# Rows gathered as three bf16 parts in a GCN and GAT kernel, from chunk 28 of pass 1 and in all of pass 2

## The chip, the core and the metric

The kernel runs on one core of a Trainium2 chip. The metric is the device time of one execution in microseconds (us), the median over the runs. Data lie in HBM; SBUF (128 partitions) and PSUM are the core's own memories. TensorE (PE) multiplies, VectorE (DVE) and ScalarE (ACT) work elementwise, GpSimd (POOL) issues the indirect DMAs that gather rows, and SyncE (SP) and ACT issue the other DMAs.

## What is computed

12500 nodes have 256 features each, and 200000 edges go from `src` to `dst`, sorted by `dst`. Two graph convolutions are followed by an output product, and then by a mix over four heads:

```python
def _gcn_conv(x, W, b, src, dst, n):        # src, dst with a self loop for each node
    h = x @ W
    dinv = where(deg > 0, rsqrt(deg), 0.0)
    msgs = h[src] * (dinv[src] * dinv[dst])[:, None]
    return segment_sum(msgs, dst, n) + b

h = relu(layernorm(x))
h = h @ W_pre + b_pre
h = relu(_gcn_conv(h, W1, b1, src, dst, n))          # pass 1
h = relu(_gcn_conv(h, W2, b2, src, dst, n))          # pass 2
x = x + h @ W_post + b_post
xt = (relu(layernorm(x)) @ weight).reshape(-1, 4, 64)
alpha = softmax(leaky_relu(alpha_l[src] + alpha_r[dst], 0.01), axis=1)
out = x + mix of xt[dst] over the heads with alpha   # of the first n edges, broadcast to the heads
```

Everything is float32.

## The kernel before

`fast_path` does the work; a general path behind it is entered only when the edges are too uneven. The instructions of each engine run in the order in which the Python code emits them.

**Tables.** A first stage (to about 130 us) writes `table1` to HBM: one row of 260 float32 for each node, 256 values, the node's scale and padding (`D1 = 260`). Pass 1 gathers rows of `table1` and writes `table2` (256 float32 a row). Pass 2 gathers rows of `table2`.

**A pass.** `convolve` does one pass. The edges are cut into 112 chunks (`NCH`) of 14 tiles (`J`) of 128 edges; there are 1563 tiles, and the last chunk has 9. For a tile, GpSimd issues one indirect DMA (L1374) that brings the 128 rows of the edges' sources into `got`, and TensorE multiplies them by a one-hot matrix (`hots[c]`, made by DVE in `one_hots`, L1241) into the sum `acc` of the chunk (tile `facc`, L1382). A float32 matmul is two instructions on PE here. At a chunk's end `close` copies the sum (`fsums`, L1276), turns it on PE, and adds it into a window of nodes `buf` (L1293). When all edges of a node tile of 128 are in, `shift` hands it to `finish`: `finish1` in pass 1, `finish2` in pass 2, for 98 node tiles (`NT`) each.

**Delayed steps.** `finish` returns a list of `(offset, step, fills)`. A step is emitted that many edge tiles later, so that PE need not wait for what comes before it. Near a pass's end (`near`, the last three chunks) the steps follow each other at one tile each. `finish1` has two steps: `d` multiplies by the folded weights, `e` applies the relu into `o` and stores it to `table2` from ACT's queue (L1422, L1423). `finish2` has nine: `d` to `h` give the node's output row and its normalized form, `i` (L1514) turns it, `k` copies it, `q` multiplies by the attention weights, `r` stores the results to `table_l`, `table_e` and `table_r`.

**Gather buffers.** A buffer (`fgot`) holds one chunk: 14 gathers. Pass 1 has five, pass 2 four. The first four chunks of pass 1 (`raw`) come from an earlier gather of `x`. A pool gives out the buffer that was released first, and the first gather into it waits for the last reader. Besides, the DMAs of GpSimd share eight semaphores in turn, so that a gather waits until the one eight before it has landed.

**Where the passes meet.** The first chunk of pass 2 (`lacking`) reads only the table's first 96 node tiles, so that it can start early; what it lacks is added by `late_sums` (L1267). That function makes two blocks of one-hots of the sources with DVE in a buffer of the gather pool (`froms`), and multiplies them by the one-hots of the targets on PE, 14 tiles for each of two node tiles, after the second edge tile. Before its first tile, pass 2 loads three broadcast rows of indices (`to_all`, L1567 and L1593), turns them into one-hots (L1572, L1595), and loads and turns the first node rows (`self`, L1200, L1206).

**The last stage.** After pass 2, 98 gathers of 16 bytes a row (`fal`, L1662) bring the attention terms, and `mix` does the softmax and the output.

Of the kernel before, what the change touches and what calls it, by code (L numbers as in the profile page):

```python
# [17 lines left out]
P = 128  # L18
# [395 lines left out]
def fast_path(  # L414
# [56 lines left out]
    table1 = dram.tile([NT * P, D1], F32, name="ftable1")  # L471
    table2 = dram.tile([NT * P, D], F32, name="ftable2")
    kept_x = dram.tile([NT * P, D], F32, name="kept_x")

# [677 lines left out]

    def convolve(ep, table, stride, width, ahead, with_sum, psum, prepare, finish, lacking=False,
                 raw=(), rows_p=None):

# [83 lines left out]
        def one_hots(h, to):  # L1239
            n = to.shape[1]  # L1240
            nc.vector.tensor_tensor(h, iota_p[:, None, :].to_broadcast([P, n, P]),  # L1241
                                    to[:, :, None].to_broadcast([P, n, P]), ALU.is_equal)

        def hot_of(c):

            n = nj[c]
            h = ep.tile([P, J, P], F32, name="fhot", bufs=3)
            one_hots(h[:, :n, :], to_0 if lacking and c == 0 else to_t[:, c, :n])
            return h

        def new_rows_of():
            if with_sum:
                return new_got()
            return rows_p.tile([P, J, stride], F32, name="fgot", bufs=ahead)

        def late_sums():

            h = ep.tile([P, J, P], F32, name="fhot", bufs=3)
            one_hots(h, to_t[:, 0, :])
            froms = new_rows_of()  # L1260
            assert stride == TW * P
            for i in range(TW):
                one_hots(froms[:, :, i * P:(i + 1) * P], from_0[:, i, :])
            px = psum.tile([P, KC, P], F32, name="fpt", bufs=1)
            for i in range(TW):
                for j in range(J):
                    nc.tensor.matmul(px[:, i, :], froms[:, j, i * P:(i + 1) * P], h[:, j, :],  # L1267
                                     start=(j == 0), stop=(j == J - 1))
            many = work.tile([P, KC, P], F32, name="fz", bufs=2)
            nc.scalar.activation(many, px, AF.Copy)  # L1270
            return many, [load_rows((NT - TW + i) * P, P) for i in range(TW)]

        def close(c, acc, t):
# [3 lines left out]
            v = {}  # L1277
            near = c + 3 >= NCH

# [19 lines left out]
            def shift(now):  # L1299
# [31 lines left out]
                for i, (o, step, fills) in reversed(list(enumerate(steps))):  # L1331
                    then = at(now + (i + 1 if near else o), lambda _, step=step: step(), fills, then)
                state["w"] += 1
# [31 lines left out]
        for t, (c, j) in enumerate(tiles):  # L1365
            if j == 0:
                acc = psum.tile([P, width], F32, name="facc", bufs=2 if not with_sum else 3)

            if j == 0:
                gots = (raw + [spare])[c] if raw and c <= len(raw) else new_rows_of()  # L1370
            got = gots[:, j, :]
            some = lacking and c == 0
            if c >= len(raw):
                nc.gpsimd.indirect_dma_start(  # L1374
                    out=got, out_offset=None, in_=table[:(NT - TW) * P, :] if some else table[:],
                    in_offset=bass.IndirectOffsetOnAxis(
                        ap=src_0[:, j:j + 1] if some else src_t[:, c, j:j + 1], axis=0))
            if j == 2 and some:
                late = late_sums()
            if j == (5 if some else 2) and c + 1 < NCH:  # L1380
                hots[c + 1] = hot_of(c + 1)
            nc.tensor.matmul(acc, hots[c][:, j, :], got[:, :width], start=(j == 0),  # L1382
                             stop=(j == nj[c] - 1 and not some))
            if some and j == nj[c] - 1:
# [5 lines left out]
            if c + 1 < len(raw):  # L1390
                raw_ahead(c + 1, j)
            run(t)
        run()
# [16 lines left out]
    def finish1(work, psum, w, buf, sbuf, fs):  # L1410
# [9 lines left out]
        def e():  # L1420
            o = work.tile([P, D], F32, name="fo", bufs=3)
            nc.scalar.activation(o, v["po"], AF.Relu, scale=dinv2[:, w:w + 1])  # L1422
            nc.scalar.dma_start(table2[w * P:(w + 1) * P, :], o)  # L1423
            if w == 8:
                late_weights(late, attn)
                first_chunk()
            if w == 9:
                check_chunks(late, psum)

        return [(6, d, fills(w, "fpo")), (10, e, None)]  # L1430

    with tc.tile_pool(name="psum1", bufs=1, space=PSUM) as psum, \
# [4 lines left out]
        convolve(ep, table1, D1, D + 1, 4, True, psum, lambda w: prepare1(work, w),  # L1437
                 lambda w, b, s, pre, _: finish1(work, psum, w, b, s, pre), raw=raw,
                 rows_p=late)
    ring.close()  # L1440
# [23 lines left out]
    def finish2(work, psum, w, buf, pre, bias):  # L1464
# [65 lines left out]
        def r():  # L1530
# [8 lines left out]
            if w < XW:  # L1539
                nc.scalar.dma_start(table_r[w * P:(w + 1) * P, :], xa[:, :DR])  # L1540

        steps = [(6, d, fills(w, "fpz")), (8, e, None), (12, f, fills(w, "fpo")), (14, g, None),
                 (16, h, None), (20, i, fills(w, "fpt")), (22, k, None),
                 (26, q, fills(w, "fpx")), (28, r, None)]
        t = w - FROM
        if 0 <= t < J:
# [11 lines left out]

            steps += [(32, ends, "fpx"), (34, copied, None)]
        return steps  # L1560
# [20 lines left out]
    with tc.tile_pool(name="psum2", bufs=1, space=PSUM) as psum, \  # L1581
            tc.tile_pool(name="fwork2", bufs=2) as work, \
            tc.tile_pool(name="edges2", bufs=1) as ep, \
            tc.tile_pool(name="fgots2", bufs=1) as rows_p:
        ep.tile([P, 320], F32, name="apart")
        for c in range(EARLY):
# [7 lines left out]
        for i in range(LW):  # L1594
            nc.vector.tensor_scalar(hot_l[i], from_all, float((NT - LW + i) * P), lane,  # L1595
                                    op0=ALU.subtract, op1=ALU.is_equal)
        convolve(ep, table2, D, D, 4, False, psum, lambda w: prepare2(work, w),
                 lambda w, b, s, pre, bias: finish2(work, psum, w, b, pre, bias), True,
                 rows_p=rows_p)

# [152 lines left out]
```

## Time and profile before

| what | us |
|---|---|
| median of 3 runs | 4152.92 (4147.09 to 4158.49) |
| the profiled execution | 4146.65, of which the span of instructions is 4144.8 |
| first gather of pass 1, first of pass 2, last of pass 2 (start) | 130.35, 2024.51, 3983.19 |
| first `fal` gather, last `fal` gather (start) | 4002.20, 4125.64 |
| busy in the span: PE, DVE, ACT, POOL | 3094.9, 1139.5, 491.0, 3105.1 |
| mean granted TensorE clock | 0.80 |

The profile names a group of instructions by line, engine, operation and `output<-inputs`. "Idle before" is the time in which the engine stood still ahead of these instructions, and the arrow names what ended it; `issue` means that nothing that the profile shows was waited for. Times in a timeline count from the span's start. The profiled execution lies 6.27 us below the median of the runs.

### The profile page before, as it was taken

The numbers are of one execution on the slowest core, as the hardware profiler recorded it, in microseconds if no ns is written. First come the engines' busy times: TensorE is split into PE (matmuls) and PEld (weight loads), VectorE is DVE, ScalarE is ACT, GpSimd is POOL, SyncE is SP. The second block draws the span as 40 slices with busy tenths as digits, with TensorE's granted clock in tenths as the row PEclk, the third lists the DMA queues.
The fourth block names the chain that finished last, engine by engine and source line by source line (L and its number), as shares of the span: only waits on it lengthen the run. The fifth ranks groups of instructions, "written<-read, shape, count | busy, mean of one in ns | idle before, by whom it ended". The sixth has DMA issues, their size and how long they took to land. (4 is left out here: it accounts for less than half of the span.)

```text
span 4144.8 us, 32267 instructions
## 1 busy us (share of the span) xinstructions
PE 3094.9 (75%) x10600; PEld 1972.5 (48%) x10600; DVE 1139.5 (27%) x2421; ACT 491.0 (12%) x1233; POOL 3105.1 (75%) x3299
## 2 busy tenths in 40 slices
PE   6697887877777878788577777777777777777774
PEld 5464444444444444444365545554555545544452
DVE  8532111111111111111232222222222222222338
ACT  5400000000000000000011111111111111111122
POOL 8677777777777777777777777777777777777766
PEclk8688778788788787777698888888888888888876
DMA  9644444444444444444544445555455445554556
GB/s 278 190 125 123 118 120 120 123 120 120 120 122 120 120 120 122 117 120 120 149 125 134 129 128 128 128 132 128 127 128 132 128 128 127 129 126 129 132 167 201
DMA packets 327419, 554.57 MB, mean 134 GB/s; under 512 B 96301, under 2 KB 224836, under 8 KB 327244
## 3 DMA queue, kind: packets, MB, share of 16 engines
q0 software_dynamic: 153520, 414.16, 38.2%
q1 hardware_dynamic: 127878, 121.99, 9.8%
q10 hardware_dynamic: 45846, 16.27, 1.6%
q8 instruction: 87, 1.43, 0.1%
q14 instruction: 88, 0.72, 0.1%
HBM read 498.89 MB, written 53.21 MB: 133 GB/s over the span
## 5 line engine op out<-in xcount | busy, mean ns | idle before, releaser
L1374 POOL DMA_INDIRECT fgot<-ftable,fsrc_t x3056 | 2892.1, 946 | 948.7 <-issue 885.3
L1382 PE MATMUL facc<-fgot,fhot 128*128 128x257 f32 (+1 forms) x6252 | 2336.0, 494 | 888.1 <-DMA fgot<-ftable,fsrc_t 845.9
L1382 PEld LDWEIGHTS facc<-fgot,fhot 128*128 128x128 f32 x6252 | 1261.1, 231 | 1803.3 <-DMA fgot<-ftable,fsrc_t 1371.6
L1293 DVE TENSOR_TENSOR buf<-buf,fturn 128x256 f32 x224 | 94.4, 422 | 1627.2 <-PE fturn L1206 1296.8
L1241 DVE TENSOR_TENSOR fhot<-iota_p,to_t 128x1792 f32<-128x1792 f32 x224 | 448.9, 2004 | 4.5 <-PE fpt L1267 4.4
L1479 DVE SCALAR_TENSOR_TENSOR fy<-rb,fb2c,fpz 128x128 f32<-128x128 f32 x194 | 58.8, 345 | 718.5 <-PE fpz L1472 717.5
L1276 ACT ACTIVATE fsums<-facc 128x257 f32<-128x257 f32 (+1 forms) x224 | 85.9, 383 | 1146.0 <-PE facc L1382 1134.5
L1493 DVE SCALAR_TENSOR_TENSOR fx<-fpo,fdinv,fxb 128x256 f32<-128x256 f32 x97 | 46.9, 484 | 506.6 <-PE fpo L1488 506.6
L1417 PE MATMUL fpo<-wf,buf 128*128 128x256 f32 x388 | 156.9, 549 | 0.3 <-DVE buf L1293 0.3
L1422 ACT ACTIVATE fo<-fpo,fdinv 128x256 f32<-128x256 f32 x97 | 45.9, 473 | 754.0 <-PE fpo L1418 752.2
L1417 PEld LDWEIGHTS fpo<-wf,buf 128*128 128x128 f32 x388 | 113.8, 294 | 29.1 <-DVE buf L1293 0.8
L1472 PE MATMUL fpz<-buf,fwb 128*128 128x128 f32 x776 | 117.2, 300 | 0.0
L1488 PE MATMUL fpo<-fwo,fz 128*128 128x256 f32 x388 | 114.8, 422 | 0.0
L1472 PEld LDWEIGHTS fpz<-buf,fwb 128*128 128x128 f32 x776 | 113.4, 221 | 2.3 <-DVE fy L1479 0.3
L1206 PE MATMUL fturn<-fident,self 128*128 128x128 f32 x396 | 85.1, 301 | 37.2 <-DMA to_all<-in_src_dram 24.5
L1662 POOL DMA_INDIRECT fal<-table_l,fsrc_t x84 | 81.3, 968 | 25.6 <-issue 22.9
L1206 PE MATMUL fturn<-fident,fsums 128*128 128x128 f32 x448 | 95.7, 299 | 0.5 <-ACT fsums L1276 0.5
L1652 PE MATMUL fends<-rows,hot_t 128*128 128x260 f32 x168 | 68.7, 582 | 32.3 <-ACT fxg L1654 31.7
L1518 ACT ACTIVATE ht<-fpt 128x256 f32<-128x256 f32 x97 | 37.1, 383 | 449.2 <-PE fpt L1514 449.1
L668 POOL DMA_INDIRECT fgot<-in_x_dram,raw_i x56 | 74.8, 1337 | 15.6 <-issue 15.6
L1418 PE MATMUL fpo<-bb,fins 2*128 2x256 f32 x194 | 85.0, 524 | 0.0
L1206 PEld LDWEIGHTS fturn<-fident,fsums 128*128 128x128 f32 x448 | 69.9, 156 | 31.0 <-issue 7.9
(267 smaller groups left out, 1723.6 us busy)
## 6 DMA issues: line engine op xcount, KB each, us to landing
fgot<-ftable,fsrc_t POOLq DMA_INDIRECT x3056
self<-ftable SPq DMA_DIRECT2D x99, 128.0 KB
self<-ftable SPq DMA_DIRECT2D x97, 130.0 KB
ftable<-fo ACTq DMA_DIRECT2D x98, 128.0 KB
kept_x<-fx SPq DMA_DIRECT2D x98, 128.0 KB
fxb<-in_x_dram SPq DMA_DIRECT2D x97, 128.0 KB
fxr<-kept_x SPq DMA_DIRECT2D x13, 896.0 KB
out_dram<-fres SPq DMA_DIRECT2D x13, 896.0 KB
```

The costliest lines, as they stand in the source:

```text
L668: nc.gpsimd.indirect_dma_start(out=raw[c][:, j, :D], out_offset=None, in_=x[:], in_offset=bass.IndirectOffsetOnAxis(ap=raw_i[:, k:k + 1], ...
L1206: nc.tensor.transpose(v["pt"][:, i * KC + k, :], rows[:, k * P:(k + 1) * P], ident)
L1241: nc.vector.tensor_tensor(h, iota_p[:, None, :].to_broadcast([P, n, P]), to[:, :, None].to_broadcast([P, n, P]), ALU.is_equal)
L1276: nc.scalar.activation(sb, acc, AF.Copy)
L1293: nc.vector.tensor_add(b, b, v["pt"][:, :KC, :])
L1374: nc.gpsimd.indirect_dma_start(out=got, out_offset=None, in_=table[:(NT - TW) * P, :] if some else table[:], in_offset=bass.IndirectOffset ...
L1382: nc.tensor.matmul(acc, hots[c][:, j, :], got[:, :width], start=(j == 0), stop=(j == nj[c] - 1 and not some))
L1417: nc.tensor.matmul(po, buf[:, k, :P], wf[:, k, :], start=(k == 0), stop=False)
L1418: nc.tensor.matmul(po, fs, bb, start=False, stop=True)
L1472: nc.tensor.matmul(pz[:, m, :], wb[:, k, m * P:(m + 1) * P], buf[:, k, :P], start=(k == 0), stop=(k == KC - 1))
L1488: nc.tensor.matmul(po, v["z"][:, m, :], wo[:, m, :], start=(m == 0), stop=(m == KC - 1))
L1662: nc.gpsimd.indirect_dma_start(out=al[:, i, :], out_offset=None, in_=(table_l if c else table_e)[:], in_offset=bass.IndirectOffsetOnAxis(a ...
```

## The change

A float32 value is written as the sum of three bf16 values (`to_parts`): the value rounded to bf16, what is left of it rounded to bf16, and what is then left. Two new tables in HBM, `parts1` (780 bf16 a row) and `parts2` (768 bf16 a row), hold these. From chunk 28 (`SINCE`) of pass 1 on and in all of pass 2 the gathers read these tables, the one-hots are bf16, and a tile takes three bf16 matmuls in place of one float32 matmul.

- `parts1` is made inside pass 1 by `split_rows`: from edge tile 70 on, at every third tile, one of the 98 node tiles is loaded from `table1` (SP), copied twice by ACT (once into PSUM, once to bf16), split by three DVE instructions, and stored (SP).
- `parts2` is made in `finish1`: `e` now does the relu in place in PSUM and copies it twice; a new step `split`, two tiles later, holds the three DVE instructions and the store on SP. `table2` stays, for the node's own rows.
- A gather buffer of these holds nine gathers (`ONE`): 36 in pass 2 in place of 56, 45 from chunk 28 of pass 1 on in place of 70. `late_sums` keeps its use of one buffer, with bf16 one-hots.
- In `finish2` the steps from `i` on come six tiles later (five for the last two), and the steps of the last four chunks, not three, follow each other at one tile each (`soon`).
- A tile that only keeps addresses apart (`apart`) grows from 320 to 3520 float32.

```diff
@@ convolve
+        def new_hot(c):
+            if since == 0:
+                return ep.tile([P, J, P], BF16, name="fhot", bufs=3)
+            h = ep.tile([P, J, P], F32, name="fhot", bufs=3)
+            if c < since:
+                return h
+            h = h.rearrange("p j n -> p (j n)").bitcast(BF16)[:, :J * P]
+            return h.rearrange("p (j n) -> p j n", n=P)
...
-            return rows_p.tile([P, J, stride], F32, name="fgot", bufs=ahead)
+            return rows_p.tile([P, ONE, 3 * stride], BF16, name="fgot", bufs=ahead)
...
-            near = c + 3 >= NCH
+            near, soon = c + 3 >= NCH, c + 4 >= NCH
...
-                    then = at(now + (i + 1 if near else o), lambda _, step=step: step(), fills, then)
+                    then = at(now + (i + 1 if soon else o), lambda _, step=step: step(), fills, then)
...
+            many = 1 if c < since else 3
+            if many == 1:
+                if j == 0:
+                    gots = (raw + [spare])[c] if raw and c <= len(raw) else new_rows_of()
+                got = gots[:, j, :]
+            else:
+                i = (t - since * J) % ONE
+                if i == 0:
+                    gots = new_rows_of()
...
+                got = gots[:, i, :]
...
+                rows_of = table if many == 1 else parts
...
-            nc.tensor.matmul(acc, hots[c][:, j, :], got[:, :width], start=(j == 0),
-                             stop=(j == nj[c] - 1 and not some))
+            for i in range(many):
+                nc.tensor.matmul(acc, hots[c][:, j, :], got[:, i * stride:i * stride + width],
+                                 start=(j == 0 and i == 0),
+                                 stop=(j == nj[c] - 1 and i == many - 1 and not some))
...
+            if behind:
+                behind(t)
@@ finish1
         def e():
-            o = work.tile([P, D], F32, name="fo", bufs=3)
-            nc.scalar.activation(o, v["po"], AF.Relu, scale=dinv2[:, w:w + 1])
+            po = v["po"]
+            nc.scalar.activation(po, po, AF.Relu, scale=dinv2[:, w:w + 1])
+            v["parts"] = work.tile([P, 3, D], BF16, name="fparts", bufs=2)
+            nc.scalar.activation(v["parts"][:, 0, :], po, AF.Copy)
+            o = work.tile([P, D], F32, name="fo", bufs=2)
+            nc.scalar.activation(o, po, AF.Copy)
             nc.scalar.dma_start(table2[w * P:(w + 1) * P, :], o)
+
+        def split():
+            to_parts(v["po"], v["parts"], parts2, w)
...
-        return [(6, d, fills(w, "fpo")), (10, e, None)]
+        return [(6, d, fills(w, "fpo")), (10, e, None), (12, split, None)]
+
+    def to_parts(p, b, table, w):
+        nc.vector.tensor_tensor(p, p, b[:, 0, :], ALU.subtract)
+        nc.vector.tensor_copy(b[:, 1, :], p)
+        nc.vector.tensor_tensor(b[:, 2, :], p, b[:, 1, :], ALU.subtract)
+        nc.sync.dma_start(table[w * P:(w + 1) * P, :], b.rearrange("p i d -> p (i d)"))
+
+    def split_rows(pool, psum):
+        rows = {}
+
+        def load(w):
+            rows[w] = pool.tile([P, D1], F32, name="frow", bufs=4)
+            nc.sync.dma_start(rows[w], table1[w * P:(w + 1) * P, :])
+
+        def step(t):
+            k, i = divmod(t - FIRST, EACH)
+            if i or not 0 <= k < NT + 2:
+                return
+            if k < NT:
+                load(k)
+            if k >= 2:
+                p = psum.tile([P, 4, P], F32, name="fpt", bufs=1)
+                p = p.rearrange("p a b -> p (a b)")[:, :D1]
+                b = pool.tile([P, 3, D1], BF16, name="frow_p", bufs=3)
+                row = rows.pop(k - 2)
+                nc.scalar.activation(p, row, AF.Copy)
+                nc.scalar.activation(b[:, 0, :], row, AF.Copy)
+                to_parts(p, b, parts1, k - 2)
+
+        return step
+
+    FIRST, EACH = (RAW + 1) * J, 3
+    SINCE = (FIRST + EACH * (NT + 2)) // J + 2
+    ONE = 9
@@ finish2
-                 (16, h, None), (20, i, fills(w, "fpt")), (22, k, None),
-                 (26, q, fills(w, "fpx")), (28, r, None)]
+                 (16, h, None), (26, i, fills(w, "fpt")), (28, k, None),
+                 (32, q, fills(w, "fpx")), (34, r, None)]
...
-            steps += [(32, ends, "fpx"), (34, copied, None)]
+            steps += [(37, ends, "fpx"), (39, copied, None)]
@@ pass 2
-        ep.tile([P, 320], F32, name="apart")
+        ep.tile([P, 3520], F32, name="apart")
```

## The prediction, made before the changed kernel had run

> **What bounds the kernel now.** I read the stages first, each engine's busy time beside the wall time. The columns after the length are PE, PEld, DVE, ACT and POOL with their counts, then PE's granted clock, DMA share and GB/s.
>
> ```profile
> 1000.00:1500.00 500.00, 393.10 (x1122) 214.87 (x1121) 89.97 (x160) 29.69 (x66) 378.15 (x401) 0.80 0.44 120
> 2050.00:2150.00 100.00, 70.06 (x316) 55.10 (x317) 35.67 (x48) 6.65 (x17) 74.26 (x78) 0.81 0.46 134
> 2700.00:3200.00 500.00, 366.20 (x1400) 257.87 (x1400) 131.76 (x284) 66.07 (x176) 378.15 (x401) 0.83 0.51 129
> 4000.00:4050.00 50.00, 42.20 (x164) 31.14 (x165) 28.98 (x55) 15.68 (x43) 36.53 (x38) 0.69 0.78 250
> ```
>
> POOL issues 401 gathers in 500 us in both passes, one each 1.247 us, although PE's work differs by 27 us, and its busy time is the same to the hundredth. That is a machine at its own pace. The costliest groups say who waits for whom:
>
> ```profile
> L1374 POOL DMA_INDIRECT fgot<-ftable,fsrc_t x3056 | 2892.1, 946 | 948.7 <-issue 885.3
> L1382 PE MATMUL facc<-fgot,fhot 128*128 128x257 f32 (+1 forms) x6252 | 2336.0, 494 | 888.1 <-DMA fgot<-ftable,fsrc_t 845.9
> L668 POOL DMA_INDIRECT fgot<-in_x_dram,raw_i x56 | 74.8, 1337 | 15.6 <-issue 15.6
> ```
>
> A gather costs 0.946 us and an "issue" gap of 0.30 us; PE stands idle 846 us until rows land. So the bound is the number of gathers. Of the 3852.8 us from the first gather (130.35) to the last (3983.19), 3069 steps of 1.249 explain 3833; 20 us are stalls. One is where the passes meet; this is its timeline:
>
> ```profile
> 2010.28 0.94 POOL L1374 DMA_INDIRECT fgot<-ftable,fsrc_t  x1 [0.30 <-issue]
> 2013.11 3.28 PE L1382 MATMUL facc<-fgot,fhot 128*128 128x257 f32 x5 [0.42 <-DMA fgot<-ftable,fsrc_t]
> ...
> 2021.23 0.33 ACTq L1423 DMA_DIRECT2D ftable<-fo  x1
> 2024.51 0.94 POOL L1374 DMA_INDIRECT fgot<-ftable,src  x1 [2.05 <-DMA ftable<-fo]
> ...
> 2033.98 0.33 ACTq L1423 DMA_DIRECT2D ftable<-fo  x1
> 2036.68 7.56 SPq L1567 DMA_DIRECT2D to_all<-in_dst_dram  x2
> ...
> 2048.75 1.68 POOL L1374 DMA_INDIRECT fgot<-ftable,fsrc_t  x1 [0.30 <-issue]
> ...
> 2071.44 3.95 DVE L1241 TENSOR_TENSOR fgot<-iota_p,from 128x1792 f32<-128x1792 f32 x2
> 2073.51 8.19 PE L1267 MATMUL fpt<-fhot,fgot 128*128 128x128 f32 x56 [1.79 <-DVE fgot L1241]
> 2081.97 0.94 POOL L1374 DMA_INDIRECT fgot<-ftable,fsrc_t  x1 [2.59 <-PE fpt L1267]
> ```
>
> The reader is to see that POOL starts pass 2 at 2024.51, but PE's first tile comes only at 2069.65, behind index loads and one-hots that begin at 2036.68, when the last store of pass 1 has landed. In between POOL fills buffers. Its 43rd gather (2081.97) needs the buffer in which `late_sums` made its source one-hots, and waits 2.59 us for the last matmul on them.
>
> **Part by part.** The sum is made against the profiled execution (4146.65; span 4144.8); the median of the runs is 6.27 above it, and I add that at the end.
>
> *Matmuls: nothing.* f32 takes 2336.0/3126 = 0.75 us of PE a tile. The nearest bf16 rows are 224 columns wide (25.1 us for 168, 0.149 each) and 512 (8.6 us for 27, 0.32); 257 columns lie near 0.17, so three cost 0.51 us. 0.24 us times 2734 tiles, 650 us of PE, is saved beside a POOL that doesn't wait for it. If POOL weren't the bound, this would be the gain.
>
> *Gather cadence: nothing.* The same 3070 gathers remain. Rows of 1560 bytes aren't in the trace. Rows of 16 bytes (`fal`) and of 1040 bytes both take 0.94 us when nothing disturbs them, so a 65-fold in bytes costs nothing; I take zero. Ends: zero, and 10% of 0.946 on 2734 gathers, +259 us, if a longer row needs more descriptors. A gain is excluded: no shorter row is cheaper.
>
> *Landing: nothing.* A gather's rows are there 2.8 us after its start (2010.28 to 2013.11), 5.3 us in the busy stretch before the last gather. Half as many bytes again make this at most 1.5-fold: 4.2 and 8 us. POOL is held only when the gather eight before hasn't landed, after 8 x 1.249 = 10.0 us. The mean DMA share goes from 0.51 to about 0.73; at 0.78 (last row of the stages) POOL still issues 38 gathers from 4002.20 on, one each 1.26 us. POOL's pace can break, though: the gathers of L668 took 1.337 us each, in the first 122 us at a share of 0.9 and with DVE busy. Ends: 0 and, if one gather for each of 97 node tiles is 0.5 us late, +49 us.
>
> The Trainium skill (DMA: Bandwidth & Descriptors, "Anatomy of one DMA — SWDGE (gpsimd) path") fits a GpSimd DMA as 2.0 us plus bytes over 436 GB/s. By that a gather would land an estimated 0.15 us later, where my bound above allows 1.4.
>
> *More frequent buffer changes: nothing.* The wait for a reader comes each 9th gather in place of each 14th. Where the reader is done, such a gather starts after the same 0.30 us (timeline at 1014.11, released by PE). PE trails by about three gathers, so 36 buffers are enough in the steady state.
>
> *`split_rows`: nothing.* Each 3.75 us: two ACT copies (0.39 each, as `fsums`), three DVE instructions (0.42 each, as L1293 and L1220), a load of 130 KB, a store of 195 KB. DVE goes from 21% to 55% there, ACT from 8% to 29%, DMA by 89 GB/s to a share near 0.8. DVE's other duty, one-hots, is emitted 12 tiles (15 us) ahead. The last `parts1` store is emitted at tile 367; the first gather from it is tile 392, 31 us later, and PE trails POOL by 3 us there. Ends 0 and +8.
>
> On SP's queue the `parts` stores wait for DVE, with `self` loads behind them that have 20 us to spare.
>
> One thing speaks against the DVE work. A DVE instruction from SBUF to SBUF at double rate lengthens a gather: the one at 2048.75 took 1.68, beside `hot_t` (L1572), 0.74 too long. The new DVE instructions read PSUM, as the adds of L1293 do, beside which gathers keep 0.95; so zero.
>
> The skill (SBUF — State Buffer, "SBUF: two separate sides") says that a DVE instruction in a two-port mode locks GpSimd out while descriptors are written; the trace agrees at 2048.75. If the 588 new ones did that at the 0.74 seen, they would cost an estimated 435 us.
>
> *Where the passes meet: +17.4 us.* `late_sums` still takes one of four buffers, the others now hold 27 gathers, not 42. So in the built program the wait for the last L1267 matmul stands at the 28th gather. I follow both sides.
> - POOL's start. Store 2021.23 becomes three ACT instructions in place of one (+0.8), three DVE (+1.3) and a larger store: first gather near 2026.6 (+2.1). 27 gathers later, with the 2.7 us that four slow ones add, POOL stands before the buffer at 2063.0.
> - PE's end. The last store of pass 1 moves by 0.8 + 1.3 less 0.4 for a quicker last tile, +1.9 with the landing (ends +1, +3); so does 2036.68. Three index loads of 896 KB beside gathers of 160 in place of 107 GB/s: 0.5 each, +1.5 (0 to +4). DVE's one-hots stay at 2.0 us each (PSUM source, one element a cycle as now). From the second source block (2075.4) PE took 6.3 us more for 56 half matmuls, still behind on the first 14 tiles; 28 bf16 ones of under 0.149 each leave 14 after the block, about 1.6 us: -4.7 (-5.2 to 0). Sum -1.3: the buffer is free at 2080.4, gather 28 starts at 2080.7, after 17.7 us of waiting where 2.6 were.
> - Gather 43 then starts 15 x 1.249 = 18.7 us later, at 2099.4, against 2081.97: +17.4 (ends +13 and +26). PE drains the landed rows at 0.5 us a tile, so the later buffers are free in time. Nothing wins this back, since POOL is the bound to the end.
>
> *The end of pass 2: -0.5.* From the last gather to the first `fal` 19.0 us pass, and POOL waits 10.6 for the last node tiles:
>
> ```profile
> 3990.69 0.95 POOL L1577 DMA_INDIRECT rows<-table_r,row_i  x1 [0.30 <-issue]
> 4002.20 0.94 POOL L1662 DMA_INDIRECT fal<-table_e,fsrc_t  x1 [10.56 <-ACT fxl L1535]
> ```
>
> 13.3 of these (3988.45, PE's last gathered tile, to 4001.75) are steps of the last two node tiles, f32 as before. The rest holds 16 f32 matmul halves, 5 us, now 3.6, against a later landing. Ends -2.4 and +2. The moved steps (`i` and `q` on PE, `k` and `r` on ACT with `r`'s two or three stores) pass six tiles' matmuls and about half a chunk's `fsums`; nothing reads them before the last stage, and `soon` keeps them out of the tail.
>
> Sum: +17.4 - 0.5 = +17, so 4163.7 for a profiled execution and 4170 for the median.
>
> **Rivals.**
> - *Faster: PE's load sets the gap.* The 0.30 us issue gap of a gather could be time that POOL loses to PE's signals. For it: 885 us stand there without a named cause. Against: it is 0.30 in both passes and in the last stage, whatever PE does. If half of it went, 2734 x 0.15 = 410 us would go: 3743. It decides from 0.01 us a gather on (27 us, more than the stall).
> - *Same: the stall is paid back.* The chain after 2036.68 runs 3 us earlier than I think and the end wins 2.4 (POOL's wait at 4002.20 is room for it): +12, 4165, within 0.3% (12.5 us, about what a measurement can tell from no change).
> - *Slower: landing reaches the eighth gather.* +49 on top: 4219.
> - *Slower: longer rows cost descriptors.* +259: 4429.
>
> **Chances.** Forecast 0.67 (own range 4164 to 4180; of it 0.09 falls within 0.3%, as runs differ by some 4 us); paid back 0.14 (0.01 faster, 0.12 same, 0.01 slower); landing 0.09; descriptors 0.05; faster 0.05, with 0.01 of it within 0.3%. So slower 0.58 + 0.01 + 0.09 + 0.05 = 0.73, same 0.22, faster 0.05. The range 4158 to 4196 leaves out the faster case, part of the second, and most of the last two, some 0.2.
>
> **What would show it.** Right: 401 gathers in each 500 us; PE's `facc` busy down by some 600 us without a change of POOL's; one wait of 15 to 20 us for L1267's successor at the 28th gather of pass 2; no wait at chunk 28. Wrong: gathers over 0.95 us in steady stretches, waits for a gather eight before, a `parts1` wait, or a POOL gap under 0.30.

## The result and the profile after

The changed kernel takes 4171.97 us (median of 20 runs, 4163.16 to 4178.01), the kernel before 4152.51 beside it: a ratio of 1.0043, with a 95% interval of 1.0035 to 1.005. That is 19.5 us more, where 17 were forecast (4171.97 against 4170). The profiled execution has a span of 4166.9, 22.1 above that of before.

The stages first, with the same columns as before (length; PE, PEld, DVE, ACT and POOL with their counts; PE's granted clock, DMA share, GB/s):

```profile
1000.00:1500.00 500.00, 355.62 (x1521) 215.81 (x1521) 123.23 (x238) 46.18 (x118) 378.12 (x401) 0.65 0.67 183
2050.00:2150.00 100.00, 54.44 (x314) 37.59 (x315) 31.85 (x39) 4.69 (x12) 61.91 (x65) 0.68 0.56 161
2700.00:3200.00 500.00, 326.67 (x1780) 244.29 (x1780) 131.84 (x284) 63.55 (x171) 378.12 (x401) 0.78 0.70 181
```

POOL issues 401 gathers in 500 us in both passes, as before, and its busy time differs by 0.03 us, though half as many bytes again move and PE works less. Only the stretch where the passes meet has lost gathers: 65, where 78 were. The groups:

```profile
L1397 POOL DMA_INDIRECT fgot<-parts,fsrc_t x2720 | 2575.4, 947 | 847.4 <-issue 798.0
L1407 PE MATMUL facc<-fgot,fhot 128*128 128x256 bf16 (+2 forms) x8986 | 1939.5, 357 | 1164.1 <-DMA fgot<-parts,fsrc_t 1084.9
```

A gather of 1560 or 1536 bytes a row takes 0.947 us, one of 1040 took 0.946. PE's gather matmuls are down by 397 us (2336.0 to 1939.5) and its idle time ahead of them is up by 276 (888.1 to 1164.1): what was saved was waited away. The place where the passes meet:

```profile
2021.56 0.95 POOL L1397 DMA_INDIRECT fgot<-parts,fsrc_t  x1 [0.30 <-issue]
2027.18 0.95 POOL L1397 DMA_INDIRECT fgot<-parts,src  x1 [4.67 <-DVE sbuf L1308]
...
2037.25 9.38 SPq L1637 DMA_DIRECT2D to_all<-in_dst_dram  x2
...
2073.85 1.46 PE L1407 MATMUL facc<-fgot,fhot 128*128 128x256 bf16 x6 [3.11 <-DVE fhot L1243]
...
2079.64 1.67 PE L1279 MATMUL fpt<-fhot,fgot 128*128 128x128 bf16 x14 [0.26 <-DVE fgot L1243]
...
2081.59 0.94 POOL L1397 DMA_INDIRECT fgot<-parts,fsrc_t  x1 [18.90 <-PE fpt L1279]
```

The last line is the 28th gather of pass 2; it waits 18.9 us for `late_sums`. The end of pass 2, and the wait of DVE in the last stage for `lacks` (the part of the attention terms that PE adds there for the last node tiles):

```profile
4010.23 0.95 POOL L1647 DMA_INDIRECT rows<-table_r,row_i  x1 [0.31 <-issue]
4019.60 0.94 POOL L1732 DMA_INDIRECT fal<-table_e,fsrc_t  x1 [8.42 <-DMA table_l<-fxl]
```

```profile
DVE fs L1738 <- PE lacks L1703: 7.0, 1, 7.0
```

The same wait in the kernel before:

```profile
DVE fs L1668 <- PE lacks L1633: 3.9, 1, 3.9
```

With these the span can be taken apart, stretch by stretch on POOL (starts of gathers, us):

| stretch | before | after | difference |
|---|---|---|---|
| start to the first gather of pass 1 | 130.35 | 128.69 | -1.7 |
| pass 1, first to last gather | 1891.2 | 1892.9 | +1.7 |
| last of pass 1 to first of pass 2 | 3.0 | 5.6 | +2.6 |
| first to 43rd gather of pass 2 | 57.5 | 73.2 | +15.7 |
| 43rd to last gather | 1901.2 | 1902.4 | +1.2 |
| last gather to first `fal` | 19.0 | 16.9 | -2.1 |
| first to last `fal` | 123.4 | 123.9 | +0.4 |
| last `fal` to the end | 19.1 | 23.4 | +4.3 |

18.3 of the 22.1 lie in the two rows where the passes meet. The last row is DVE's: it waits 7.0 us for `lacks` where it waited 3.9, so that its last instruction ends 20.5 later though the last `fal` starts 17.8 later, and the last store takes 8.0 us in place of 6.4. Two single executions are set side by side here; rows of a few us are no more than that.

One thing must be known for the experiments. Eleven of the twelve ran on three other chips, on which the kernel before takes 4925 to 4931 us. There PE often issues only one matmul in 0.7 to 2.8 us with nothing to wait for, falls some 70 us behind POOL, and POOL gets 340 to 350 gathers through in 500 us (1000 to 1500 and 2700 to 3200 us), since it waits for buffers. A total from there answers how the changes compare on such a chip, not what they are worth where POOL runs free. But at the start of pass 2 the buffers are empty and POOL runs at its own pace on those chips too, so the stretch from the first to the 43rd gather can be compared. The last run was on a chip like the first, with before at 4152.97. The changed kernel was measured on only one of the three other chips, together with the run "loads late, `fal` early"; for the other runs the distance to it in total time is one between chips. What is read from traces comes from one execution of each run.

### The profile page after: what moved, and what is told of

It is laid out like the page before. It is cut to its first block, busy times and chain, and to the rows that moved or that the text cites. A ratio compares the mean times of both kernels' runs of the same rounds, so it can differ in the third digit from the quotient of the medians.

```text
span 4166.9 us, 38958 instructions
## 1 busy us (share of the span) xinstructions
PE 2792.7 (67%) x13306; PEld 1908.1 (46%) x13306; DVE 1387.1 (33%) x3009; ACT 620.5 (15%) x1625; POOL 3104.4 (75%) x3299
## 5 line engine op out<-in xcount | busy, mean ns | idle before, releaser
L1397 POOL DMA_INDIRECT fgot<-parts,fsrc_t x2720 | 2575.4, 947 | 847.4 <-issue 798.0
L1407 PE MATMUL facc<-fgot,fhot 128*128 128x256 bf16 (+2 forms) x8986 | 1939.5, 357 | 1164.1 <-DMA fgot<-parts,fsrc_t 1084.9
L1407 PEld LDWEIGHTS <-fhot 128*128 128x128 bf16 x8202 | 984.7, 122 | 1737.2 <-issue 1468.0
L1243 DVE TENSOR_TENSOR fhot<-iota_p,to_t 128x1792 bf16<-128x1792 f32 (+1 forms) x224 | 449.0, 2005 | 0.0
L1397 POOL DMA_INDIRECT fgot<-ftable,fsrc_t x336 | 318.5, 948 | 117.7 <-issue 103.1
L1468 DVE TENSOR_TENSOR fpo<-fpo,fparts 128x256 f32<-128x256 f32 x97 | 41.8, 431 | 928.4 <-ACT fo L1454 928.4
L1549 DVE SCALAR_TENSOR_TENSOR fy<-rb,fb2c,fpz 128x128 f32<-128x128 f32 x194 | 58.8, 345 | 674.6 <-PE fpz L1542 674.6
L1407 PEld LDWEIGHTS facc<-fgot,fhot 128*128 128x128 f32 x784 | 160.1, 222 | 134.2 <-DMA fgot<-ftable,fsrc_t 84.0
L1542 PE MATMUL fpz<-buf,fwb 128*128 128x128 f32 x776 | 170.1, 393 | 1.0 <-DVE buf L1305 1.0
L1542 PEld LDWEIGHTS fpz<-buf,fwb 128*128 128x128 f32 x776 | 164.1, 311 | 7.0 <-DVE buf L1305 1.2
L1445 PEld LDWEIGHTS fpo<-wf,buf 128*128 128x128 f32 x388 | 106.8, 300 | 48.6 <-DVE buf L1305 28.6
L1450 ACT ACTIVATE fpo<-fpo,fdinv 128x256 f32<-128x256 f32 x97 | 43.2, 445 | 574.5 <-PE fpo L1446 574.5
L1558 PE MATMUL fpo<-fwo,fz 128*128 128x256 f32 x388 | 110.9, 412 | 0.7 <-ACT fz L1552 0.6
```

The lines of the kernel that those rows point to most:

```text
L1397: nc.gpsimd.indirect_dma_start(out=got, out_offset=None, in_=rows_of[:(NT - TW) * P, :] if some else rows_of[:], in_offset=bass.IndirectOf ...
L1407: nc.tensor.matmul(acc, hots[c][:, j, :], got[:, i * stride:i * stride + width], start=(j == 0 and i == 0), stop=(j == nj[c] - 1 and i == ...
L1445: nc.tensor.matmul(po, buf[:, k, :P], wf[:, k, :], start=(k == 0), stop=False)
L1542: nc.tensor.matmul(pz[:, m, :], wb[:, k, m * P:(m + 1) * P], buf[:, k, :P], start=(k == 0), stop=(k == KC - 1))
L1549: nc.vector.scalar_tensor_tensor(y[:, m, :], v["root"], b2c[:, m:m + 1], v["pz"][:, m, :], op0=ALU.mult, op1=ALU.add)
L1558: nc.tensor.matmul(po, v["z"][:, m, :], wo[:, m, :], start=(m == 0), stop=(m == KC - 1))
```

## The experiments

The changed kernel itself, on one of those chips:

> The changed kernel itself, once more, so that the experiments have it beside them on their chip. Theory: where POOL keeps 401 gathers in 500 us, the 28th gather of pass 2 waits 19 us and the time is 17 to 21 above before; where engines stop now and then for longer than 0.3 us (350 gathers in 500 us, as in the two calls before), the order of these stops decides as much as the stall, and it lies within 40 us of before on either side.

4938.66 against 4925.13, ratio 1.0017 (1.0 to 1.0033). Two lines of its POOL timeline, and PE's largest wait:

```profile
686.74 0.95 POOL L1397 DMA_INDIRECT fgot<-parts,fsrc_t  x1 [46.11 <-DMA fins<-root_t]
...
2452.25 0.94 POOL L1397 DMA_INDIRECT fgot<-parts,fsrc_t  x1 [14.17 <-PE fpt L1279]
```

```profile
PE facc L1407 <- issue: 1094.7, 1090, 3.8
```

The second is the 28th gather of pass 2; it waits 14.2 us here, since POOL's start comes later against PE's. The first is the first gather from `parts1` (tile 392). The release is put down to a small DMA, but it comes 3.2 us after the last instruction of `split_rows` on DVE ends (683.56), and the gather has to wait for the `parts1` stores, the last of which is issued there. PE is 60 us behind POOL at this tile, ACT and DVE serve PE's tiles in order, and so the last store is late. On the first chip PE trailed by 3 us, the last split ended 24.5 us before this gather (533.56 and 558.06), and the wait was not there.

What the others show where the passes meet (us from the first gather of pass 2; starred rows are from chips of the first kind):

| run | PE's first tile | `late_sums` ends | longest wait, at gather | 43rd gather |
|---|---|---|---|---|
| before* | 45.1 | 57.2 | 2.6, 43rd | 57.5 |
| after* | 46.7 | 54.1 | 18.9, 28th | 73.2 |
| after, other chip | 42.6 | 50.1 | 14.2, 28th | 69.2 |
| parts in pass 2 alone | 44.5 | 52.0 | 16.0, 28th | 71.0 |
| parts in pass 1 alone | 41.1 | 59.6 | 4.6, 43rd | 59.8 |
| nine f32 gathers a buffer | 41.2 | 54.3 | 18.3, 28th | 73.3 |
| late sums apart | 44.1 | 51.6 | 6.5, 37th | 61.8 |
| five buffers | 34.8 | 42.2 | 4.2, 37th | 58.8 |
| loads late | 26.2 | 33.7 | 5.2, 28th | 57.4 |
| loads late, `fal` early | 26.0 | 33.4 | 5.2, 28th | 57.4 |
| first part alone | 39.6 | 47.1 | 11.0, 28th | 66.1 |
| before, loads late | 22.1 | 60.9 | 8.9, 43rd | 61.2 |
| before, both edits | 22.2 | 60.7 | 8.6, 43rd | 61.0 |
| both edits, nine f32* | 26.9 | 39.5 | 6.3, 28th | 59.3 |

**Parts in pass 2 alone.**

```diff
-                 ... parts1, SINCE, raw=raw, rows_p=late, behind=split_rows(late, psum))
+                 ... parts1, NCH, raw=raw, rows_p=late)
```

> Parts only in pass 2: pass 1 gathers f32 rows of table1 to its end, split_rows and parts1 are not there, finish1 still makes parts2. Theory (all of the loss arises where the passes meet, because late_sums holds one of four buffers of nine): the 28th gather of pass 2 waits 18 to 19 us for the last L1279 matmul, and the time is that of the changed kernel, 4171 (4168 to 4174), 18 to 19 above before. Rival (part of the loss is made inside pass 1 by the split work on DVE and ACT and by the longer rows there): the same wait at the boundary, but the last gather of pass 1 starts 2 us or more before 2021.5, and the time is 4162 to 4167.

4895.30 against 4927.67, ratio 0.9938 (0.9916 to 0.9961). Where the passes meet (the boundary), it is as the theory has it: a wait of 16.0 at the 28th gather. The total is not: it is 43 less than the changed kernel's on the other such chip, near to the 46.1 that the changed kernel waits for `parts1`. So on these chips pass 1's part costs, as the rival says; that it does so by that one wait, which the prediction had priced at 0 to 8 us, fits but rests on single executions.

**Parts in pass 1 alone** (pass 2, `finish1` and the delayed steps as before):

> Parts only in pass 1 (split_rows, parts1, bf16 matmuls from chunk 28 on); pass 2, finish1 and the delayed steps are those of the kernel before. Theory (pass 1's parts cost and bring nothing): the last gather of pass 1 at 2021.5 (2021 to 2023), the 43rd gather of pass 2 near 2082 after a wait of 2 to 3 us, time 4152.5 to 4155. Rival (pass 1's parts cost 5 us or more, by slow gathers or a wait for parts1 at chunk 28): 4158 or more, with the last gather of pass 1 after 2026. Rival (fewer PE cycles help): under 4148.

4957.84, ratio 1.0059 (1.004 to 1.0078), 30 more than before. The wait at the first `parts1` gather is 28.6, and again the gather starts 3 us after `split_rows` ends. Pass 2's 43rd gather waits 4.6. The rival with the wait at chunk 28 holds on these chips. The traces of all the runs there say the same: from the first gather of pass 1 to the first of pass 2 the four with f32 rows in pass 1 took 2218 to 2227 us, the seven with parts 2248 to 2278.

They also show where the 32 us of "parts in pass 2 alone" come from. From the first gather of pass 2 to the end, the six runs there with three parts took 2527 to 2550 us, the three with fourteen f32 gathers a buffer 2559 to 2587. On these chips pass 2 gains by the change in spite of the stall; why was not tested.

**Nine f32 gathers a buffer** (the kernel before, pass 2):

```diff
-            if j == 0:
+            i = j if with_sum else t % 9
+            if i == 0:
                 gots = (raw + [spare])[c] if raw and c <= len(raw) else new_rows_of()
-            got = gots[:, j, :]
+            got = gots[:, i, :]
```

> The kernel before with one edit: in pass 2 a buffer is left after nine gathers in place of fourteen (four of them: 36 gathers in place of 56); rows, matmuls and late_sums stay f32. Theory (the number of gathers between two uses of the buffer that late_sums holds sets the loss, and bf16 has no part in it): the 28th gather of pass 2 waits for the last L1267 matmul until about 2081.7, some 20 us, the 43rd starts near 2100.5 in place of 2081.97, and the time is 4171 (4168 to 4174). Rival (the longer bf16 rows and the steps added to finish1 make the loss): 4153 to 4160. Rival (the first 14 tiles' f32 matmuls make the next buffers late as well): a second wait at the 37th gather, 4175 or more.

4885.01, ratio 0.9914 (0.9892 to 0.9936). The boundary line:

```profile
2408.59 0.94 POOL L1375 DMA_INDIRECT fgot<-ftable,fsrc_t  x1 [18.30 <-PE fpt L1267]
```

The stall is there in full without any bf16: 18.3 us at the 28th gather, the 43rd after 73.3 us as in the changed kernel (73.2). So fewer gathers ahead of the buffer are enough to make it. The total went the other way by 43 us (4885.01 against 4927.67), which no theory expected; why smaller buffers gain on a chip where PE holds POOL stays open.

**Late sums apart** (the source one-hots in a tile of their own):

```diff
-            froms = new_rows_of().rearrange("p j d -> p (j d)")[:, :J * D]
-            froms = froms.rearrange("p (j d) -> p j d", d=D)
+            froms = ep.tile([P, J, D], BF16, name="froms", bufs=1)
```

> The changed kernel with the source one-hots of late_sums in a tile of their own (bf16, taken from the space of apart), so that the four buffers hold 36 gathers. Theory: the wait moves to the 37th gather, which needs the first buffer, so the matmul of tile 9; that stands on PE behind late_sums (end 2081.3) and six tiles of 0.5 to 0.8 us, so 2084.3 to 2086.1. POOL stands there at 2074.3; the wait is 10 to 12 us, and the 37th gather starts at 2084.6 to 2086.4 in place of 2092.8: 6.5 to 8 us less than the changed kernel, 4164 to 4165.5. Rival (it is late_sums' use of a buffer alone that costs): no wait above 1 us, 4153. Rival (the stall is PE's late start and is as long wherever it is met): 4172.

```profile
2447.35 0.94 POOL L1396 DMA_INDIRECT fgot<-parts,fsrc_t  x1 [6.54 <-PE facc L1406]
```

4918.21, ratio 0.9981 (0.9966 to 0.9997). The wait moved to the 37th gather and to the gather matmuls, 2.7 us (six tiles of 0.44) after the late sums end, and the 43rd gather came 7.4 us earlier than in the changed kernel on such a chip; 6.5 to 8 were expected. The wait itself is 6.5 us where 10 to 12 were expected from a stall of 18.9; on such a chip the stall is 14.2. The total is 20 less, but on another chip, and the single runs of the two overlap.

**Five buffers** (`apart` from 3520 to 64 f32, `ahead` from 4 to 5):

> The changed kernel with a fifth buffer of nine gathers in pass 2 (in the space of apart). Theory: nine more gathers, 11.2 us, pass before POOL meets the buffer of late_sums: the wait for L1279 is at the 37th gather and is 7.5 to 8.5 us long, and the time is 11.2 us less than the changed kernel's, 4160 to 4162. Rival (PE's backlog then holds the next buffers, so the stall only moves): a further wait for L1407 of some us at the 46th gather, 4165 to 4172.

4924.64, ratio 0.9988 (0.9968 to 1.0008), 14 less than the changed kernel. The wait at the 28th gather is gone, and the 43rd comes 10.4 us earlier. But the wait of 4.2 us at the 37th is not for `late_sums`, which had ended five us before it began: PE began 8 us earlier against POOL in this run. So the length of the remaining wait says little. That the stall left the 28th, and that no wait stands at the 46th where the rival had put one, speak for the theory; the earlier start of PE accounts for some of the gain.

**Loads late.** The three index loads and five one-hots, at tiles 30 to 72:

```diff
-        for c in range(EARLY):
-            turn_hots(ap, c, load_ends(work, c, 1), EARLY)
...
+        def ends_later(t):
+            k, i = divmod(t - 30, 15)
+            if i == 0 and k in range(EARLY):
+                ends_0[k] = load_ends(work, k, 1)
+            if i == 12 and k in range(EARLY):
+                turn_hots(ap, k, ends_0[k], EARLY)
...
-                 True, rows_p=rows_p)
+                 True, rows_p=rows_p, behind=ends_later)
```

> The changed kernel with the three index loads (to_all) and the five one-hots made from them (hot_t, hot_l) moved from the start of pass 2 to edge tiles 30 to 72 of it; only the last stage and a late step read them. Theory: PE's late start is these loads. Node rows (self) are loaded at 2037.3 at once, land by 2041, PE's first tile comes near 2051 in place of 2073.85, late_sums ends near 2059, and the 28th gather (2063) doesn't wait: 17 to 19 us less than the changed kernel, 4153 to 4155. Rival (PE's start is set by the node rows and the copies after them, or by the one-hots): 5 to 10 us less, a wait of 9 to 14 us left at the 28th gather. Rival (the loads and the DVE work cost as much in their new place): 4160 or more, with slow gathers after 2070.

```profile
2435.06 1.46 PE L1407 MATMUL facc<-fgot,fhot 128*128 128x256 bf16 x6 [3.11 <-issue]
...
2440.86 1.68 PE L1279 MATMUL fpt<-fhot,fgot 128*128 128x128 bf16 x14 [0.26 <-DVE fgot L1243]
...
2447.49 0.94 POOL L1397 DMA_INDIRECT fgot<-parts,fsrc_t  x1 [5.21 <-remote]
```

4919.53, ratio 0.9981 (0.9964 to 0.9998), 19 less than the changed kernel on the other such chip. PE's first tile comes 26.2 us after POOL's first gather (2408.84) in place of 42.6, `late_sums` ends at 2442.54, and POOL arrives at 2442.3. What is left, 5.2 us to a release that the profile can't place ("remote"), starts when PE's part is done by the profile; an ACT and a DVE instruction behind the same matmuls go on only at 2447.25, so PE's signal seems to come late there (argued from these two lines, not tested). The 43rd gather comes 11.7 us earlier, not 17 to 19, since the stall was 14.2 and not 18.9 on such a chip.

**First part alone.** In pass 2 `parts2` holds the first part, 512 bytes a row, and a tile has one matmul, so the output lacks what the other two parts add:

> The changed kernel without the second and third parts in pass 2: parts2 holds the first part alone (512 bytes a row in place of 1536), a tile has one bf16 matmul in place of three; the output lacks what the other two parts add. Theory (POOL's own pace sets both passes): 401 gathers in each 500 us of pass 2, the wait at the 28th gather stays, shorter by the 3 to 4 us that the index loads take less beside lighter gathers, and the time is 4166 to 4170. Rival (bytes or PE's signals set the 0.30 us gap or a part of the 0.946): if 0.05 us or more of a gather goes, 75 us or more, under 4095.

```profile
2700.00:3200.00 500.00, 185.27 (x846) 137.68 (x846) 116.58 (x251) 49.99 (x140) 328.42 (x349) 0.61 0.30 67
```

The same stretch of the changed kernel on the other such chip:

```profile
2700.00:3200.00 500.00, 276.28 (x1491) 192.48 (x1491) 112.66 (x240) 50.39 (x137) 325.45 (x344) 0.68 0.59 156
```

4904.84, ratio 0.9941 (0.9918 to 0.9964). 349 gathers pass in 500 us where the changed kernel had 344. A third of a gather's bytes (67 GB/s in all in place of 156) and a third of the matmuls bring 34 us, 0.7%. A gather takes 0.945 us still, with the same 0.30 between two that wait for nothing. The rival by which PE's signals or bytes set POOL's pace would have given over 75. The 401 gathers expected could not come here, since POOL waits for PE on this chip. The wait at the 28th gather is 11.0 us in place of 14.2, 3.2 shorter beside lighter gathers, as expected (3 to 4).

**Before, loads late** (the same edit to the kernel before):

> The kernel before with the same move of the index loads and their one-hots to edge tiles 30 to 72 of pass 2. Theory: its wait at the 43rd gather, 2.59 us with 0.3 of it there anyway, goes, and nothing else: 2 to 3 us less than before, 4149.5 to 4150.5, too little for the interval. Rival (PE's late start costs more than the one wait shows, by later buffers or the clock): 5 us or more, under 4147.5. Rival (the loads collide with pass 2's other transfers): over 4152.5.

```profile
2389.54 0.37 PE L1267 MATMUL fpt<-fhot,fgot 128*128 128x128 f32 x1 [1.83 <-issue]
2392.34 0.37 PE L1267 MATMUL fpt<-fhot,fgot 128*128 128x128 f32 x1 [2.43 <-issue]
2395.14 0.37 PE L1267 MATMUL fpt<-fhot,fgot 128*128 128x128 f32 x1 [2.43 <-issue]
```

4928.60, ratio 1.0 (0.9977 to 1.0024). PE began 22.1 us after POOL, but one of the slow stretches of these chips fell on `late_sums`: a matmul of 0.37 us each 2.8 us, so that it took 35 us and the 43rd gather waited 8.9. Inconclusive for what was asked.

**Loads late, `fal` early**, on the changed kernel and on the kernel before:

```diff
+    fals = [ap.tile([P, G, H], F32, name="fal", bufs=4) for i in range(4)]
...
-            al = mp.tile([P, G, H], F32, name="fal", bufs=4)
+            al = fals[g % 4]
```

> The changed kernel with two edits. One: the three index loads and the five one-hots from them move from the start of pass 2 to its edge tiles 30 to 72. Two: the four fal buffers of the last stage come from space that is not used before it, so that the first fourteen fal gathers wait only for table_e. Theory for the first: PE's first tile comes some 22 us earlier, the 28th gather doesn't wait, 17 to 19 us less than the changed kernel at the 43rd gather. Theory for the second: the first fal gather follows the last gather of rows at once (8 us earlier against the last gather of pass 2 than in the changed kernel), DVE's first softmax 5 to 7 us earlier, and the end 3 to 7. Together 20 to 26 us less than the changed kernel, 0 to 7 less than before. Rival for the first (PE's start is set by the node rows): 5 to 10 us of it. Rival for the second (PE's lacks or DVE hold the last stage anyway): nothing from it, the waits on lacks grow by as much.

> The kernel before with both edits: the index loads and their one-hots at edge tiles 30 to 72 of pass 2, and the four fal buffers in space that is not used before the last stage. Theory: where POOL runs free, the first edit is worth the 2.3 us of the wait at the 43rd gather; by the second the first fal gather starts when the last store of table_e has landed, near 3993 in place of 4002.2, and the end comes 3 to 7 us earlier: 5 to 9 us less than before, under both kernels. Where PE holds POOL (350 gathers in 500 us, PE 56 gathers behind), the first edit is worth nothing that shows, and the second 5 to 15 us of the 44 to 52 that POOL waits there for the last node tiles. Rival (PE's lacks and DVE hold the last stage): first fal as early, its later gathers wait for DVE, the end within 2 us of before.

The first took 4919.66, ratio 0.9991 (0.9978 to 1.0003), 19 less than the changed kernel on the same chip: the boundary repeats that of the loads alone (57.4), and last gather to first `fal` went from 52.8 to 37.4 us, but the time from first to last `fal` grew by 5.3. The second took 4919.86, ratio 0.9975 (0.9954 to 0.9996); PE's slow stretch lay on `late_sums` again (8.6 us of wait), and `fal` came only 3 us earlier than without that edit, since PE, 56 gathers behind, was late with the last node tiles.

**Both edits and nine f32 gathers a buffer**, the only run on a chip of the first kind:

> The kernel before with the index loads late, the fal buffers in free space, and buffers left after nine gathers in pass 2, as in the run nine_f32. It asks why nine_f32 was 43 us under before although its 28th gather waits 18 us. Theory: the waits at the buffer changes themselves. PE's pace holds POOL there, a buffer of nine comes free sooner than one of fourteen, and less is queued behind PE when a pass ends; then the gain comes again, 4870 to 4890. Rival: the places at which PE issues one matmul in 2.8 us fall differently in each program; then the time is that of the run with both edits, 4900 to 4940. In either case PE's first tile of pass 2 comes 19 us after the first gather, and the 28th gather doesn't wait for L1267 unless such a stretch falls into it. Where POOL runs free: 5 to 9 us less than before.

```profile
2054.19 2.08 PE L1383 MATMUL facc<-fgot,fhot 128*128 128x256 f32 x4 [3.10 <-DVE fhot L1241]
...
2058.05 8.76 PE L1267 MATMUL fpt<-fhot,fgot 128*128 128x128 f32 x56 [1.79 <-DVE fgot L1241]
...
2067.08 0.94 POOL L1375 DMA_INDIRECT fgot<-ftable,fsrc_t  x1 [6.33 <-PE fpt L1267]
```

4150.22 against 4152.97, ratio 0.9991 (0.9981 to 1.0): 2.8 us less, where 5 to 9 were expected. It can't answer its question on the 43 us, as POOL runs free here (401 gathers in 500 us). It answers another: with as few gathers ahead as the changed kernel, and PE's first tile 26.9 us after POOL's first gather in place of 46.7, the stall at the 28th gather is 6.3 us in place of 18.9. PE starts later than the 19 us expected, and f32 `late_sums` takes 8.8 us where bf16 took 3.6; with the bf16 kernel's 7.4 us from PE's first tile to their end the buffer would be free 34.3 us after the first gather, about 1 us after POOL comes (an estimate, not run there). The early `fal` gathers brought next to nothing: the first starts 12.7 us after the last gather in place of 19.0, but DVE waits 6.9 us for `lacks` where it waited 3.9, and from the last gather to the end are 160.6 us, before 161.6. Its time is below that of both kernels; that it is below the kernel before is not shown, since the interval reaches 1. No run on a chip of the first kind takes the stall out of the changed kernel itself; that this would bring back some 18 us there follows from its trace, but was not measured.

## Why the prediction was right, point by point

The forecast, +17 by one wait where the passes meet, came true in its place, its cause and nearly its size. The rival in which the stall is paid back (+12) lies below the measured interval, which begins at 14.5 us; the one in which landing reaches the eighth gather (+49) lies above it.

- **Gather cadence: right.** 401 in 500 us, 0.947 us each with the 0.30 us gap. The rivals of PE's load (3743) and of descriptors (4429) are out. A third of the bytes on another chip left the gather at 0.945.
- **Matmuls worth nothing: right; the term of the saving was mis-sized.** 650 us of PE were forecast, 397 came. The bf16 forms took 1692.4 us for 2734 tiles, 0.62 each, not 0.51. The three matmuls of a tile take 0.49 us at best, but the granted clock fell from 0.80 to 0.73 over the span and to 0.65 in the middle of pass 1, and there the same three take 0.80 us more often than 0.49. Two lines of PE's timeline show both, and behind them two rows of stages around these lines, where the clock (behind POOL's column) is 1.00 and 0.50:

```profile
1015.76 0.49 PE L1407 MATMUL facc<-fgot,fhot 128*128 128x257 bf16 x3 [1.70 <-DMA fgot<-parts,fsrc_t]
...
1020.34 0.80 PE L1407 MATMUL facc<-fgot,fhot 128*128 128x257 bf16 x3 [0.42 <-DMA fgot<-parts,fsrc_t]
```

```profile
1015.50:1016.40 0.90, 0.49 (x3) 0.29 (x3) 0.00 (x0) 0.00 (x0) 0.59 (x2) 1.00 0.74 213
1020.20:1021.30 1.10, 0.80 (x3) 0.41 (x3) 0.00 (x0) 0.00 (x0) 0.80 (x2) 0.50 0.51 156
```

- **Landing: right in effect.** The median grew from 2.8 to 3.2 us in pass 1 and to 3.6 in pass 2, within the bound of 4.2; the longest between 2110 and 3900 us is 6.3, and no gather waited for the one eight before. The estimate from the Trainium skill (DMA: Bandwidth & Descriptors, "Anatomy of one DMA — SWDGE (gpsimd) path"), 0.15 us later, is too small by a factor of three to five; the measurement decides.
- **`split_rows`: right on the first chip alone.** No wait at tile 392 there. The 31 us from the emission of the last store to its first reader are what PE's lag eats into: with a lag of 3 us, 24.5 were left from the last split to the gather, and where PE lags 60 us the wait is 46. The step had that number in it (PE trails POOL by 3 us) and took it as fixed.
- **DVE against POOL: right.** The DVE instructions that read PSUM left the gathers at 0.947. The one-hots between SBUF tiles lengthen three gathers at the boundary to 1.5 to 1.7 us; in the kernel before there were four, of 1.4 to 1.8. The estimate of 435 us by the Trainium skill's rule on two-port modes (SBUF — State Buffer, "SBUF: two separate sides") had asked what would be if the new instructions cost gathers as much; their gathers show no such cost.
- **Where the passes meet: right, 18.4 for 17.4.** POOL's start came +2.7 (forecast +2.1; the line at 2027.18 names DVE's L1308, but by the trace the store of `parts2` issued at 2024.42 landed at 2026.28, 0.90 us before the gather, and the store before the change landed 0.94 us before its gather), gather 28 at 2081.6 (2080.7) after 18.9 us (17.7), gather 43 at 2100.35 (2099.4). Two terms missed in opposite directions, so that part of the closeness is luck: the stores of pass 1 delayed the index loads by 0.6, not 1.9, since the last node tiles found PE at a higher clock (0.95 in place of 0.50 from 2026 us on; 1.13 us in place of 2.07 for four matmuls); and the three loads beside heavier gathers cost 3.6, not 1.5. The shorter `late_sums`, -4.6, were forecast at -4.7. The run with nine f32 gathers a buffer shows that fewer gathers ahead make the stall without any bf16, and the one with loads late that PE's late start behind those loads is the other condition: without it 5.2 us of 14.2 were left. Both were run on the other chips, and their stalls compared there.
- **The end of pass 2: right in sign.** -2.1, forecast -0.5.
- **Not in the sum:** the last stage, +4.7 in the one execution (`lacks` and the last store), against which stands that the medians differ by 19.5 and not 22.1.

## What to carry to other kernels

Before a matmul is made cheaper, look at who sets the pace: one row per stage with the counts of instructions is enough, and POOL's 401 before and after said it. Where a wait is small today, work out how many steps of the bounding engine lie ahead of it, because a buffer that holds fewer of them turns the rest of the distance into a stall. And a producer's margin is a distance to a consumer plus its lag: check it against the largest lag that may occur, not the one of a single chip.

## What the runs showed of the hardware

- With three bf16 matmuls in place of an f32 one, the clock granted fell: the steady stages of the changed kernel got 0.65 and 0.78 of the clock where those of before got 0.80 and 0.83, and PE was busy for less time (356 and 327 us of 500 in place of 393 and 366). With a single bf16 matmul a tile, on another chip, the clock was lower again, 0.61 with PE busy for 185 us, where the changed kernel on such a chip had 0.68 with 276. So the runs don't separate the bf16 form from PE's longer idle time as the cause. Of the unchanged f32 steps in pass 2, L1542 went from 0.300 to 0.393 us a matmul, but L1558 from 0.422 to 0.412.
- The pace of a 128-row indirect DMA from GpSimd did not depend on the bytes of a row between 16 and 1560: undisturbed it took 0.94 to 0.947 us and a gap of 0.30. Longer ones stood beside DVE's one-hots between SBUF tiles (1.4 to 1.8 us) and in the first stage (L668, 1.337 us each in the kernel before).
- The same kernel took 4153 us on one kind of chip and 4925 to 4931 on three others. There PE's largest idle item is "issue" (1094.7 us in the changed kernel; on the first chip landings ended such time, 1084.9 us), matmuls come one in 0.7 to 2.8 us for 20 to 30 us at a stretch, and gathers land earlier than on the first chip (2.55 us in place of 2.77 for f32 rows). A third of the matmuls and of the bytes together changed the pace by 1.5% (349 gathers in 500 us, 344 before). What holds PE back there was not found.
